# Four entries ordered by gathers through HBM, and the perceptron's bias and mask on TensorE and ScalarE

## The chip, the cores and the metric

The kernel runs on one core of one Trainium2 chip. The time is the device time of one execution in microseconds; the median of several executions is given. The profile is that of one execution.

## What is computed

There are 16 graphs ("entries") of 1024 nodes with 64 features, and a dense weighted adjacency matrix for each. Four layers follow one another; each adds its result to x and normalises the 64 features.

```
layer 0: messages = adj @ x;  dh = tanh([x, messages] @ W1 + b1) @ W2 + b2
layer 1: (adj / rowsum(adj)) @ x
layers 2, 3: neighbours are thinned by their rank, symmetrically
         for each node and feature, over the values of its remaining neighbours:
             agg = 0.25*quantile(.25) + 0.5*quantile(.5) + 0.25*quantile(.75)
         y = (relu((x + agg) @ W1 + b1) @ W2 + b2) * mask
after each layer: x = layernorm(x + result)
```

## The kernel before

The work of an entry is split into stages, each a Python generator. `features` does layers 0 and 1 on TensorE from adjacency columns that SyncE loads 512 KB at a time, twice per entry. `cuts` finds the neighbours to be removed. `lists` makes the reduced neighbour matrix, counts each node's neighbours and ranks the nodes by that count; `order` is the permutation as a 0/1 matrix of 1024 x 1024. All later work is on nodes in this order, so that the nodes of one tile of 128 have similar counts and tile t needs at most SIZES[t] values for each node.

Still in `lists` (L802 to L865) every tile but the last is packed: for tile t the rows of the neighbour matrix that belong to it are selected with `order` (16 matmuls of 512 columns, L861 to L863, after two that add a position term, L860), and from the result `pk` ScalarE and VectorE read off the neighbours' numbers, `e.idx`. The last tile (`by_pick`) is packed the other way round (L851 to L855). `ordered` (L867) selects each node's count, number and mask with `order` (`ps`), orders x2 with 192 matmuls on a three-part bf16 copy of it (`pick`, L882 to L886, from `x2p` made by `split` in `features`, L637 to L639), copies the result to `x2s` and stores it in a DRAM table.

`fetch` then gathers, with one indirect DMA of GpSimd for each list position, 128 rows of that table into a ring of 60 slots, `got_s`. VectorE sorts the slots by compare-exchange steps, ScalarE scales the wanted ones by quantile weights (`weigh`), TensorE adds them up. For the last tile and the longest lists, TensorE selects the values with 0/1 matrices instead (`mark_picks`, `fill`: hot, pgk). A round takes two entries through one layer; the 16 rounds are (layer, pair) = (0,0), (0,1), (1,0), (0,2), (1,1), (0,3) and so on. `finish` (L1162) is a round's end for one entry: four groups of two tiles through the perceptron, then the layer norm, then the table of the next layer or the scatter of the output.

The order of the instructions on VectorE, ScalarE and TensorE is that in which the generators issue them. `Weave` always resumes the generator whose next time is earliest, on the clock of `Clocks`, a planner with fixed costs for each engine (L238) that keeps when each tile is written and read; `landed` and `vacant` hold a generator back until the plan says that data is there or room is free. `clocks.put` also charges the queues of SyncE and GpSimd. The engines themselves work through their queues in order and wait on semaphores. Entries are prepared one after another; `allowed` lets the preparation run ahead of the rounds, first to entry 4.

Two lines that the text refers to:

```
L884  pick(px[:, t, :], order[:, :, t * P : (t + 1) * P], e.x2p)
L1184 dve.tensor_add(y[:, g : g + 2], pd, b2r[:, None, :].to_broadcast([P, 2, C]))
```

In the profile every instruction of this part stands under L301, the line of the wrapper that records it, so groups are told apart by their tiles.

Of the kernel before, what the change touches and what calls it, by code (L numbers as in the profile page):

```python
# [22 lines left out]
P = 128  # L23
# [13 lines left out]
HALVINGS = 0  # L37
ROOM = 60
BY_PICK = 6
LONG = 40  # L40
BIG = 1e30
EPS = 1e-5
# [283 lines left out]
def adj_resnorm_kernel(ctx: ExitStack, tc: tile.TileContext, x, adj_t, nodemask, w01, b01, w02, b02,  # L326
                       w21, b21, w22, b22, w31, b31, w32, b32, out):
    nc = tc.nc
    B, N, C = x.shape
    NT = N // P  # L330
# [5 lines left out]
    s = SimpleNamespace()  # L336
# [38 lines left out]
        nc.vector.memset(ends_of[:, i : i + 1], float(value))  # L375
    one_f = const.tile([P, 1], F32, name="one_f")
    nc.vector.memset(one_f, 1.0)
    eps = const.tile([P, 1], F32, name="eps")
    nc.vector.memset(eps, EPS)
    nth = const.tile([P, 1], F32, name="nth")  # L380
# [90 lines left out]

    table = [[dram.tile([N + 1, C], F32, name=f"table{layer}{i}") for i in range(TABLES)] for layer in range(2)]
    table_t = dram.tile([C, N], F32, name="table_t")
    with tc.tile_pool(name="last_row", bufs=1) as last_row:
        no_row = last_row.tile([1, C], F32, name="no_row")
        nc.vector.memset(no_row, BIG)
        for tab in table[0] + table[1]:
            nc.sync.dma_start(tab[N : N + 1, :], no_row)
# [66 lines left out]
    def features(b, e):  # L545
# [32 lines left out]
        for h in range(NH):  # L578
# [6 lines left out]
            for q in range(G):  # L585
                t = h * G + q
# [47 lines left out]
        yield from settle(x2, y, "x")  # L634
        while b and entries[b - 1].xs[0] is None:
            yield
        parts = s.feat.tile([P, NT, 3, C], BF, name="x2p", bufs=1)  # L637
        yield from split(x2, parts, y)
        e.x2p = parts  # L639
# [79 lines left out]
    def lists(b, e):  # L719
# [29 lines left out]
        for t in range(NT + 1):  # L749
            if t:  # L750
                bank, pv = pvs[t - 1]
                nc.scalar.activation(left(t - 1), pv, AF.Relu, accum_out=key[:, 4, t - 1 : t], saturate=False)
                read_big[bank] = True
            if t < NT:
                rows = slice(t * P, (t + 1) * P)
                bank, pv = yield from big("pv")
                pvs.append((bank, pv.rearrange("p (c n) -> p c n", n=P)))
                for h in range(NH):
                    wide = slice(h * HALF, (h + 1) * HALF)
                    nc.tensor.matmul(pv[:, wide], minus_i, takes[:, t, wide], start=True, stop=False)  # L760
                    for c in range(h * G, (h + 1) * G):
                        cols = slice(c * P, (c + 1) * P)
                        nc.tensor.matmul(pv[:, cols], near[:, c, rows], ident_b, start=False, stop=False)
                        nc.tensor.matmul(pv[:, cols], takes[:, c, rows], minus_i, start=False, stop=c == (h + 1) * G - 1)
            yield
# [33 lines left out]

        e.idx = s.feat.tile([P, LINKS[-1]], I32, name="idx", bufs=6)  # L800
        pks, codes, found = {}, {}, {}
        for t in (*reversed(range(NT)), -1, -2, -3, -4):  # L802
            done = t + 4
            if done in found:
# [43 lines left out]
            if t >= 0:  # L848
                rows = slice(t * P, (t + 1) * P)
                bank, pk = pks[t] = yield from big("pk")  # L850
                if t in e.by_pick:  # L851
                    for q in range(NT):
                        for c in range(NT):
                            nc.tensor.matmul(pk[:, q * P : (q + 1) * P], left(c, q), order[:, c, rows],
                                             start=c == 0, stop=c == NT - 1)  # L855
                else:
                    for h in range(NH):
                        wide = slice(h * HALF, (h + 1) * HALF)
                        cols = pk[:, wide].rearrange("p (q n) -> p q n", n=P)
                        nc.tensor.matmul(pk[:, wide], first_ones, minus_at[:, wide], start=True, stop=False)  # L860
                        for c in range(NT):  # L861
                            nc.tensor.matmul(cols, order[:, c, rows], left(c, slice(h * G, (h + 1) * G)), start=False,
                                             stop=c == NT - 1)  # L863
                e.packed = t == 0
            yield  # L865

    def ordered(b, e, order, own):  # L867
# [9 lines left out]
        sorted_own = s.work.tile([P, NT, 3], F32, name="sorted_own", bufs=1)  # L877
        nc.scalar.copy(sorted_own, ps)
        count = sorted_own[:, :, 0]
        while e.x2p is None:  # L880
            yield
        px = s.psum.tile([P, NT, C], F32, name="ordered_x", tag="s", bufs=1)  # L882
        for t in range(NT):
            pick(px[:, t, :], order[:, :, t * P : (t + 1) * P], e.x2p)  # L884
            if t % 2:
                yield  # L886
        e.out_rows = s.feat.tile([P, NT], I32, name="out_rows", bufs=8)
        dve.tensor_scalar(e.out_rows, sorted_own[:, :, 1], float(b * N), None, op0=ALU.add)
        e.mask = s.feat.tile([P, NT], F32, name="mask_s", bufs=8)
        dve.tensor_copy(e.mask, sorted_own[:, :, 2])  # L890
        yield
        while b >= 4 and entries[b - 4].xs[1] is None:
            yield
        e.xs[0] = s.feat.tile([P, NT, C], F32, name="x2s", bufs=4)
        nc.scalar.copy(e.xs[0], px)
        nc.sync.dma_start(table[0][b % TABLES][:N, :].rearrange("(t p) c -> p t c", p=P), e.xs[0])
        weave.add(parted(b, e, 0))
        places = {}
# [263 lines left out]
    def finish(m, b, e, layer, agg, spare=False):  # L1162

        xc = e.xs[layer]
        w1s, b1c, w2s, b2r = mlps[layer]
        own, wide = ("y_x", "node_in") if spare else ("y_m", "o_t")

        y = s.work.tile([P, NT, C], F32, name="y_m", tag=own, bufs=1)
        own_rows = slice(m * C, (m + 1) * C)
        for g in range(0, NT, 2):  # L1170
            if spare:
                bank = s.psum.tile([P, N], F32, name="m_o", tag="big", bufs=2)
            else:
                bank = s.psum.tile([P, HALF], F32, name="m_o", tag="m", bufs=1)
            ph, pd = bank[:, : 2 * P], bank[:, 2 * P : 3 * P].rearrange("p (g c) -> p g c", c=C)
            nc.tensor.matmul(ph[:H], w1s[own_rows], agg[own_rows, g : g + 2, :], start=True, stop=True)
            yield
            h_t = s.work.tile([H, 2 * P], F32, name="h_t", tag=wide, bufs=1)
            nc.scalar.activation(h_t, ph[:H], AF.Relu, bias=b1c)
            yield  # L1180
            for q in range(2):
                nc.tensor.matmul(pd[:, q, :], h_t[:, q * P : (q + 1) * P], w2s, start=True, stop=True)
            yield
            dve.tensor_add(y[:, g : g + 2], pd, b2r[:, None, :].to_broadcast([P, 2, C]))  # L1184
        dve.tensor_mul(y, y, e.mask[:, :, None].to_broadcast([P, NT, C]))
        dve.tensor_add(y, y, xc)
        tag, bufs = ("x3s", 4) if layer == 0 else ("x2s", 4) if spare else ("x4s", 1)
        xn = s.feat.tile([P, NT, C], F32, name="xn", tag=tag, bufs=bufs)
        yield from settle(xn, y, "x" if spare else "m")
        yield  # L1190
        if layer == 0:
            nc.sync.dma_start(table[1][b % TABLES][:N, :].rearrange("(t p) c -> p t c", p=P), xn)
            e.xs[1] = xn
            weave.add(parted(b, e, 1))
            return
        for t in range(NT):
            put = nc.gpsimd.indirect_dma_start(
                out=out_rows_of, out_offset=bass.IndirectOffsetOnAxis(ap=e.out_rows[:, t : t + 1], axis=0),
                in_=xn[:, t, :], in_offset=None)
            tc.declare_no_dep(put.ins, group=f"rows{b}", reason="they write different rows")  # L1200
            tc.add_to_no_dep_group(f"rows{b}", put.ins)
# [43 lines left out]
    def landed(*aps):  # L1245
        while clocks.when(*aps) > clocks.now:
            yield clocks.when(*aps) + SLACK

    def quiet(engine, ahead=0.5):
        while clocks.free[engine] > clocks.now + ahead:  # L1250
            yield clocks.free[engine] - ahead / 2

    entries = [SimpleNamespace(near=None, st=None, cut=False, taken=False, packed=False, listed=None, there=None, by_pick=(NT - 1,), place6=None, seated=(), placed=False, counted=False, x2p=None, place=None, none=None,
                               wts=None, parts=[None, None], xs=[None, None], filled=[False, False], ends=None) for _ in range(B)]
    for e in entries:
        e.listed, e.there, e.seated = set(), {}, set()
# [462 lines left out]
```

## Time and profile before

| | |
|---|---|
| median of 3 runs | 7080.39 us (7067.44 to 7087.93) |
| the profiled execution | 7089.6 us, its span 7087.9 us |
| mean granted TensorE clock | 0.721 |
| gathers into the ring (POOL) | 2872, 1027 ns each |
| x2s written, entries 0 to 3 | at 179, 444, 700 and 926 us |
| x2s written, entries 4 and 5 | at 1327 and 1559 us |
| mask multiplied in finish, round 0 | at 929 and 1053 us |
| the same, round 1 | at 1676 and 1802 us |

PE is TensorE's matmuls, PEld its weight loads, which overlap them; DVE is VectorE, ACT ScalarE, POOL GpSimd, SP SyncE. A group in the profile is written out<-in with the names of the tiles, and x is the number of instructions. A float32 matmul stands as two instructions. Busy shares are means over the whole run. In waits, "issue" is idle time for which the profile shows no cause, and "remote" a release that it can't attribute. Some matmul records can be missing from a trace.

### The profile page before, as it was taken

How to read it: one execution, taken by the hardware profiler on the slowest of the kernel's cores; microseconds unless marked ns; L12 is line 12 of the kernel's file. 1: busy time of each engine (PE TensorE's matmuls, PEld its weight loads, DVE VectorE, ACT ScalarE, POOL GpSimd, SP SyncE). 2: the span in 40 equal slices, each digit the busy share in tenths (PEclk: the TensorE clock that was granted, in tenths of full speed). 3: DMA queues.
4: the chain of work that ended last, by engine and by line, in shares of the span. 5: the costliest groups of instructions: out<-in, count | busy, mean ns of one | idle time of the engine just before them, and what ended most of it. 6: DMA issues, size and time to landing. Idle time of an engine off the chain costs nothing.

```text
span 7087.9 us, 127458 instructions
## 1 busy us (share of the span) xinstructions
PE 4478.5 (63%) x51916; PEld 3422.8 (48%) x51916; DVE 4036.7 (57%) x8753; ACT 3112.9 (44%) x7225; POOL 3090.2 (44%) x3096
## 2 busy tenths in 40 slices
PE   7678676776665767566675656657666566454354
PEld 5446444554544545454544535545555454353344
DVE  2447345574654747556564655638465477375646
ACT  4446444454434445444443444445343444233233
POOL 0432225535254454544455354544445454455540
PEclk8678776776776867777776767768677677666667
DMA  2212212221111211111121211201111010001100
GB/s 79 49 38 60 53 44 49 51 50 20 36 45 24 57 21 46 40 40 41 24 51 29 52 27 30 56 18 39 44 42 32 16 20 16 17 18 21 18 15 5
DMA packets 414449, 253.93 MB, mean 36 GB/s; under 512 B 103434, under 2 KB 365850, under 8 KB 413850
## 3 DMA queue, kind: packets, MB, share of 16 engines
q0 software_dynamic: 96000, 98.50, 7.8%
q1 hardware_dynamic: 317850, 147.19, 7.3%
q8 instruction: 408, 6.68, 0.4%
q14 instruction: 191, 1.56, 0.1%
HBM read 232.88 MB, written 12.59 MB: 35 GB/s over the span
## 4 chain that ended last, share of the span: by engine, by line
PE 41%; issue 21%; DVE 15%; ACT 12%; another core or an unknown queue 9%; POOL 1%; DMA 0%; DVEq 0%; ACTq 0%; POOLq 0%
PE pgk L301 19%; PE pk L301 7%; DVE other L301 6%; DVE got_s L301 4%; PE pa L301 3%; ACT junk L301 2%; ACT hot L301 2%; DVE got L301 2%; PE px L301 2%; PE pr L301 2%; PE m_o L301 2%; ACT got_s L301 2%; PE ordered_x L301 1%; ACT got L301 1%
## 5 line engine op out<-in xcount | busy, mean ns | idle before, releaser
L301 POOL DMA_INDIRECT got_s<-table,idx x2872 | 2948.2, 1027 | 3707.0 <-DVE other L301 1096.4
L301 PEld LDWEIGHTS <-hot 128*128 128x128 bf16 x26304 | 1172.9, 112 | 1686.2 <-issue 1480.2
L301 PE MATMUL pgk<-x1p,hot 128*128 128x64 bf16 x13152 | 709.3, 216 | 692.1 <-issue 499.8
L301 PE MATMUL pgk<-x0p,hot 128*128 128x64 bf16 x13152 | 693.0, 214 | 676.9 <-issue 545.4
L301 DVE TENSOR_SCALAR hot<-place 128x1024 bf16<-128x1024 f16 (+1 forms) x824 | 320.8, 428 | 974.4 <-remote 769.3
L301 PEld LDWEIGHTS <-order 128*128 128x128 bf16 x7008 | 392.1, 105 | 520.0 <-issue 384.9
L301 ACT COPY got<-pgk 64x192 f32<-64x192 f32 (+2 forms) x600 | 182.5, 305 | 994.7 <-PE pgk L301 797.5
L301 ACT COPY agg<-pgk 128x128 f32<-128x128 f32 (+2 forms) x183 | 44.3, 242 | 1164.8 <-PE pgk L301 708.1
L301 PE MATMUL pk<-near,order 128*128 128x512 fp8e4 x1760 | 490.3, 418 | 55.2 <-issue 51.9
L301 DVE TENSOR_TENSOR other<-got_s 128x512 f32<-128x512 f32 (+10 forms) x826 | 491.5, 607 | 13.4 <-DVE hot L301 0.3
L301 PE MATMUL pgk<-ident,got_s 128*64 128x128 f32 x2904 | 425.4, 326 | 89.8 <-ACT got L301 36.2
L301 PEld LDWEIGHTS <-near 128*128 128x128 fp8e4 x4224 | 300.1, 109 | 302.9 <-issue 301.5
L301 PEld LDWEIGHTS pgk<-ident,got_s 128*64 128x64 f32 x2904 | 386.9, 167 | 119.9 <-ACT got L301 41.2
L301 ACT ACTIVATE got_s<-got_s,wts 128x64 f32<-128x64 f32 x1540 | 391.1, 335 | 95.0 <-DVE got_s L301 86.5
L301 DVE TENSOR_TENSOR got_s<-other 128x512 f32<-128x512 f32 (+9 forms) x719 | 391.4, 559 | 8.2
L301 DVE TENSOR_TENSOR got_s<-got_s 128x512 f32<-128x512 f32 (+9 forms) x638 | 373.0, 589 | 20.8 <-ACT got_s L301 5.4
L301 PE MATMUL pa<-x,adj_r 128*128 128x65 f32 x2048 | 331.5, 320 | 78.4 <-issue 70.9
L301 PEld LDWEIGHTS pa<-x,adj_r 128*128 128x128 f32 x2048 | 318.9, 238 | 92.1 <-issue 85.5
L301 ACT ACTIVATE code<-pk,ends_of 128x1024 f16<-128x1024 f32 x220 | 235.4, 1106 | 255.7 <-PE pk L301 113.2
L301 DVE TENSOR_TENSOR other<-other 128x128 f32<-128x128 f32 (+10 forms) x617 | 323.1, 524 | 17.8
L301 ACT ACTIVATE junk<-pr,nb_st 128x1024 fp8e4<-128x1024 f32 x256 | 284.7, 1112 | 72.7 <-remote 34.5
L301 ACT ACTIVATE hot<-hot,one_f 128x1024 bf16<-128x1024 bf16 x272 | 312.3, 1148 | 8.9
(211 smaller groups left out, 7779.9 us busy)
## 6 DMA issues: line engine op xcount, KB each, us to landing
adj_r<-in_adj_dram SPq DMA_DIRECT2D x256, 512.0 KB
got_s<-table,idx POOLq DMA_INDIRECT x2872
x_s<-in_x_dram SPq DMA_DIRECT2D x16, 256.0 KB
table<-x2s SPq DMA_DIRECT2D x16, 256.0 KB
table<-xn SPq DMA_DIRECT2D x16, 256.0 KB
out_dram<-xn,out_rows POOLq DMA_INDIRECT x128
table<-no_row SPq DMA_DIRECT2D x12, 0.2 KB
w21s<-in_L_gnn_W_dram SPq DMA_DIRECT2D x2, 32.0 KB
```

The costliest lines, as they stand in the source:

```text
L301: return call(*args, **kwargs)
```

## The change

For the first four entries (EARLY = 4) the selection of rows by matmuls with `order` is replaced by gathers through HBM, in two places. The reduced neighbour matrix is stored to DRAM (`left_d`), one store of 128 KB for each of its 8 parts, in runs of 128 bytes; the sorted node numbers are made an index (`from_rows`); for each tile but the last, one indirect DMA fetches its 128 rows of 1 KB, two tiles ahead, and one matmul for each half with the identity brings them into `pk` beside the position term. x2 is stored to DRAM (`x2_d`), and 8 indirect DMAs write `x2s` directly. The three-part split and the 192 matmuls for these entries are gone.

In `finish`, for all entries and both layers, the perceptron's second bias is added by a float32 matmul with one contraction row (`ones_row` and one row of the bias) that opens the accumulation for each tile; the mask is multiplied by ScalarE as it copies each tile out of PSUM. The two VectorE steps (the addition of the bias for each group, the multiplication by the mask for the entry) are gone.

```
@@ features
+        if b < EARLY:
+            nc.sync.dma_start(x2_d[b].rearrange("(t p) c -> p t c", p=P), x2)
+            e.x2p = x2
+            return
         parts = s.feat.tile([P, NT, 3, C], BF, name="x2p", bufs=1)
         yield from split(x2, parts, y)
@@ lists
                 nc.scalar.activation(left(t - 1), pv, AF.Relu, accum_out=key[:, 4, t - 1 : t], saturate=False)
+                if b < EARLY:
+                    to = left_d[b][(t - 1) * P : t * P, :]
+                    nc.sync.dma_start(to.rearrange("p (q n) -> p q n", n=P // 4), left(t - 1).bitcast(F32))
...
+        def fetch_row(t):
+            gather(fetched_rows[:, t % 2], left_d[b], e.from_rows[:, t : t + 1])
+        if b < EARLY:
+            fetched_rows = s.feat.tile([P, 2, N // 4], F32, name="fetched_rows", tag="x3s", bufs=4)
+            while e.from_rows is None:
+                yield
...
+                    if b < EARLY:
+                        yield from landed(fetched_rows[:, t % 2])
                     for h in range(NH):
                         nc.tensor.matmul(pk[:, wide], first_ones, minus_at[:, wide], start=True, stop=False)
+                        if b < EARLY:
+                            nc.tensor.matmul(pk[:, wide], ident_b, fetched_rows[:, t % 2].bitcast(F8)[:, wide], start=False, stop=True)
+                            continue
                         for c in range(NT):
                             nc.tensor.matmul(cols, order[:, c, rows], left(c, slice(h * G, (h + 1) * G)), start=False,
                                              stop=c == NT - 1)
+                if b < EARLY:
+                    if t == NT - 1:
+                        fetch_row(t - 1)
+                        fetch_row(t - 2)
+                    elif t > 1:
+                        fetch_row(t - 2)
@@ ordered
+        if b < EARLY:
+            e.from_rows = s.feat.tile([P, NT], I32, name="from_rows", bufs=2)
+            dve.tensor_copy(e.from_rows, sorted_own[:, :, 1])
...
+        if b >= EARLY:
+            px = s.psum.tile([P, NT, C], F32, name="ordered_x", tag="s", bufs=1)
+            for t in range(NT):
+                pick(px[:, t, :], order[:, :, t * P : (t + 1) * P], e.x2p)
...
+        if b >= EARLY:
+            nc.scalar.copy(xs, px)
+        else:
+            yield from landed(x2_d[b][:])
+            for t in range(NT):
+                gather(xs[:, t, :], x2_d[b], e.from_rows[:, t : t + 1])
+            yield from landed(xs)
@@ finish
             for q in range(2):
-                nc.tensor.matmul(pd[:, q, :], h_t[:, q * P : (q + 1) * P], w2s, start=True, stop=True)
-            yield
-            dve.tensor_add(y[:, g : g + 2], pd, b2r[:, None, :].to_broadcast([P, 2, C]))
-        dve.tensor_mul(y, y, e.mask[:, :, None].to_broadcast([P, NT, C]))
+                nc.tensor.matmul(pd[:, q, :], ones_row, b2r[:1], start=True, stop=False)
+                nc.tensor.matmul(pd[:, q, :], h_t[:, q * P : (q + 1) * P], w2s, start=False, stop=True)
+            yield
+            for q in range(2):
+                nc.scalar.activation(y[:, g + q, :], pd[:, q, :], AF.Copy, scale=e.mask[:, g + q : g + q + 1])
+        yield
```

More of the change, by code (lines that the diff above doesn't have):

```diff
@@ L39 @@
 BY_PICK = 6
+EARLY = 4
 LONG = 40
@@ L377, in adj_resnorm_kernel @@
     nc.vector.memset(one_f, 1.0)
+    ones_row = const.tile([1, P], F32, name="ones_row")
+    nc.vector.memset(ones_row, 1.0)
     eps = const.tile([P, 1], F32, name="eps")
@@ L473, in adj_resnorm_kernel @@
     table_t = dram.tile([C, N], F32, name="table_t")
+    left_d = [dram.tile([N, N // 4], F32, name=f"left_d{b}") for b in range(EARLY)]
+    x2_d = [dram.tile([N, C], F32, name=f"x2_d{b}") for b in range(EARLY)]
     with tc.tile_pool(name="last_row", bufs=1) as last_row:
@@ L879, in ordered @@
         count = sorted_own[:, :, 0]
-        while e.x2p is None:
-            yield
[L882 to L886, printed above, removed]
+        if b < EARLY:
+            e.from_rows = s.feat.tile([P, NT], I32, name="from_rows", bufs=2)
+            dve.tensor_copy(e.from_rows, sorted_own[:, :, 1])
         e.out_rows = s.feat.tile([P, NT], I32, name="out_rows", bufs=8)
@@ L890, in ordered @@
         dve.tensor_copy(e.mask, sorted_own[:, :, 2])
+        while e.x2p is None:
+            yield
[3 more added lines that the diff above has]
+                pick(px[:, t, :], order[:, :, t * P : (t + 1) * P], e.x2p)
+                if t % 2:
+                    yield
         yield
@@ L893, in ordered @@
             yield
-        e.xs[0] = s.feat.tile([P, NT, C], F32, name="x2s", bufs=4)
-        nc.scalar.copy(e.xs[0], px)
+        xs = s.feat.tile([P, NT, C], F32, name="x2s", bufs=4)
+        if b >= EARLY:
[5 more added lines that the diff above has]
+            yield from landed(xs)
+        e.xs[0] = xs
         nc.sync.dma_start(table[0][b % TABLES][:N, :].rearrange("(t p) c -> p t c", p=P), e.xs[0])
@@ L1181, in finish @@
             for q in range(2):
-                nc.tensor.matmul(pd[:, q, :], h_t[:, q * P : (q + 1) * P], w2s, start=True, stop=True)
+                nc.tensor.matmul(pd[:, q, :], ones_row, b2r[:1], start=True, stop=False)
+                nc.tensor.matmul(pd[:, q, :], h_t[:, q * P : (q + 1) * P], w2s, start=False, stop=True)
             yield
-            dve.tensor_add(y[:, g : g + 2], pd, b2r[:, None, :].to_broadcast([P, 2, C]))
-        dve.tensor_mul(y, y, e.mask[:, :, None].to_broadcast([P, NT, C]))
+            for q in range(2):
+                nc.scalar.activation(y[:, g + q, :], pd[:, q, :], AF.Copy, scale=e.mask[:, g + q : g + q + 1])
+        yield
         dve.tensor_add(y, y, xc)
@@ L1251, in quiet @@
             yield clocks.free[engine] - ahead / 2
-    entries = [SimpleNamespace(near=None, st=None, cut=False, taken=False, packed=False, listed=None, there=None, by_pick=(NT - 1,), place6=None, seated=(), placed=False, counted=False, x2p=None, place=None, none=None,
+    entries = [SimpleNamespace(near=None, st=None, cut=False, taken=False, packed=False, listed=None, there=None, by_pick=(NT - 1,), place6=None, from_rows=None, seated=(), placed=False, counted=False, x2p=None, place=None, none=None,
                                wts=None, parts=[None, None], xs=[None, None], filled=[False, False], ends=None) for _ in range(B)]
```

## The prediction

> **What bounds the kernel now.** I read the page first, then the waits, then the start of the run in the chain and in windows, because the larger half of the change acts only there.
>
> ```profile
> PE 4478.5 (63%) x51916; PEld 3422.8 (48%) x51916; DVE 4036.7 (57%) x8753; ACT 3112.9 (44%) x7225; POOL 3090.2 (44%) x3096
> ...
> PE 41%; issue 21%; DVE 15%; ACT 12%; another core or an unknown queue 9%; POOL 1%; DMA 0%; DVEq 0%; ACTq 0%; POOLq 0%
> ```
>
> No engine looks full, but the chain runs over PE for 41%, and 21% is "issue", time without a visible cause. The waits say whose it is (engine, releaser, total us, times, longest):
>
> ```profile
> POOL got_s L301 <- DVE other L301: 1096.4, 74, 87.7
> PE pgk L301 <- issue: 1088.6, 1293, 10.1
> ...
> DVE hot L301 <- remote: 769.3, 93, 54.0
> ...
> PE pgk L301 <- ACT got L301: 383.2, 140, 29.8
> DVE y_m L301 <- PE m_o L301: 334.9, 66, 25.3
> ```
>
> PE's waits on named others are 664 us for ACT and 234 us for DVE in the whole run, 13% of 7088. The rest of its idle time, 1638 us, is "issue". So PE is held by its own stream for about 87% of the span, while DVE and ACT stand behind it (DVE waits 335 us for the perceptron's matmuls alone). Two windows at the start show what such "issue" time is:
>
> ```profile
> core 0: us, PE busy (x) PEld busy (x) DVE busy (x) ACT busy (x) POOL busy (x), PEclk, DMA share, GB/s
> 149.00:195.00 46.00, 46.00 (x461) 28.42 (x459) 20.34 (x32) 23.98 (x35) 5.99 (x7) 1.00 0.21 56
> 196.00:254.00 58.00, 5.05 (x40) 3.31 (x39) 0.00 (x0) 0.28 (x1) 38.67 (x41) 0.53 0.14 24
> ```
>
> From 149 to 195 us, entry 0 is put in order: PE is full at clock 1.00, POOL hardly works. From 196 POOL gathers back to back (41 in 58 us), PE gets 40 matmuls through, ACT and DVE nothing. The trace gives no cause, but the neighbourhood is plain: a gather can cost PE up to 58/41 = 1.4 us. On average it is at most 1638/3000 = 0.55 us (2872 gathers, 128 scatters).
>
> The chain from 150 us gives the prices of what is removed:
>
> ```profile
> 150.03 1.40 PE ordered_x L301 x48
> 151.44 1.00 PE px L301 x2
> 152.44 4.30 PE pk L301 x18
> ```
>
> One block of 18 matmuls packs one tile of an entry; four blocks of 48 order x2.
>
> **What the Trainium skill says.** "TensorE: Matmul & The Clock Gate", section "LDWEIGHTS (loading the stationary operand)": the load's time goes by columns, not by rows of the contraction. The trace agrees: m_o's weights of 64 rows load in 182 ns at least, those of 128 rows in 186. So a bias matmul with a single row is priced as a full one. Its section "Architectural detail: the array is 16× 32×32, not 1× 128×128": matmuls keep program order, only weight loads are pulled ahead; so one that waits for a fetched row holds all behind it. The window from 196 us agrees at least in that nothing else got past. "DMA: Bandwidth & Descriptors", "Anatomy of one DMA — SWDGE (gpsimd) path": about 2 us fixed, mostly the write's receipt, HBM the heaviest. Here the 256 KB store of table (issued 181.47) let the first gather go at 187.18, 5.7 us later, so I use 5.7. Its "Specifications": full rate needs 512 bytes or more; the new stores have runs of 128 bytes, and no run here shows such a store.
>
> **The change, part by part.** The sum is made against the profiled execution, 7089.6 us (span 7087.9 and 1.7 around it), which is 9 us above the median of 7080.4; the difference is then taken from the median.
>
> *Packing of entries 0 to 3.* Seven tiles each, 28 in all, go from 18 matmuls to 4. At 4.30 us per 18, 4 cost 0.96; saved 3.34 x 28 = 94 us at full clock. The granted clock from 0 to 930 us, in which these four entries are prepared, is 0.77: 94/0.77 = 121 us of PE.
>
> *Ordering of x2.* Four blocks of 1.40 us per entry: 5.6 x 4 = 22 us, 29 at 0.77. The split of x2 goes too: 3 copies of 0.62 us on ACT, 2 subtractions of 0.69 on DVE, 13 us in all. Costed at nothing: from 0 to 930 us ACT is 51% and DVE 45% busy, behind PE; 13 us if PE no longer covers it.
>
> *Gathers.* 7 rows of 1 KB and 8 of x2 per entry, 60 in all. On POOL 1.25 us apart (0.94 and a gap of 0.30): 75 us on an engine busy for 236 of those 930. Their price on PE isn't known for these shapes: between 0 and 1.4 us each, 0 to 84 us; by the bytes (28 of them carry four times the usual) 0 to 144 x 1.4 = 202. A gain is excluded, since nothing shows PE faster beside gathers. I take 0.55 x 60 = 33, because most come singly between packing steps, not in bursts of 40.
>
> *Stores.* 36 more DMAs on SP, 32 of 128 KB and 4 of 256. An adjacency load queued behind a left_d store waits for ACT's Relu. Loads run two tiles ahead, and PE waited for one DMA, 9.7 us once, at the start. Cost 0; if that cover goes, a few us for each of 32. The x2_d store lands long before its gathers.
>
> *New waits on PE.* A tile's matmul waits for its row. Behind it stand features, picks and cuts of other entries in PE's queue, and behind PE stand ACT and DVE. Rows are fetched two tiles ahead; a tile takes about 8 us now (152.44, 159.17, 167.20, 174.79 in the chain), so a fetch has some 12 us. The store is over by then, and I take 5.7 us as enough for gather and landing: hidden, 0. Ends: 0 to 8.5 us for each row of entries 1 to 3 (below). For x2s, 8 gathers (10 us) and 5.7 stand in place of 25 us of picking: no loss. Waiting for from_rows before the first tile adds the ps matmuls and two copies, 2 us, under other work.
>
> Start, together: -121 - 29 + 33 = -117 us of PE, times the 0.87 that PE carries: **-102**.
>
> *Bias on PE.* From the last round:
>
> ```profile
> 7043.91 1.10 PE L301 MATMUL m_o<-w32s,h_t 128*128 128x64 f32 x8 [0.62 <-ACT h_t L301]
> 7044.67 0.29 DVE L301 TENSOR_TENSOR y_m<-m_o,b32r 128x128 f32<-128x128 f32 x1 [1.69 <-PE m_o L301]
> ```
>
> That line has two entries' group of two tiles: 8 instructions, 4 per entry, 0.55 us. The bias adds as many: 4 groups x 0.55 = 2.2 us in a finish, 70 in 32 at full clock, 98 at the mean clock of 0.721; I take 84. 22 finishes lie before 5800 us (0.87 carried), 10 after it, where PE is only half busy (0.5): 84 x (0.69 x 0.87 + 0.31 x 0.5) = **+63**. Bounds 35 and 98.
>
> *Bias and mask off DVE, onto ACT.* DVE loses 128 x 0.29 + 32 x 0.69 = 59 us and, more, its stand before m_o (335 us, and part of 169 put down to "remote"). ACT gets 256 scalings at 0.25 us (8 in 2.0 us in the last layer norm), 64 us, and that stand. Behind DVE's stand were sorting and picks' marks; behind ACT's are the emptying of pick banks and scaled rows. PE waits 234 us for DVE and 664 for ACT, so the swap lies between -234 and some +100 (15% of 664). DVE also feeds POOL's slots (1096 us). I take **-15**.
>
> *The very end.* Four groups get 0.5 us on ScalarE and 0.55 on PE for one DVE add of 0.29 (about +0.75 each), and the mask's 0.69 goes: **+2**.
>
> Sum: -102 + 63 - 15 + 2 = -52: 7038 for the profiled execution, **7028** for the median. What is late next: still PE, now with perceptron work spread over all rounds.
>
> **Rivals.**
> *The rows come late* (slower, 7122). POOL works in order too, and waits 14.8 us on average (1096.4/74) for a sort to free a slot; a fetch behind such a wait stops PE. Of the lead of 12 us the gather takes 5.7, so 14.8 - 6.3 = 8.5 us are left; for every second of the 21 rows of entries 1 to 3 that is 11 x 8.5 = +94. It decides from 52/8.5, six rows. For: POOL's long waits. Against: in entry 0 POOL has nothing else, and slots are freed by the work that PE has already passed.
> *The start doesn't set the pace* (slower, 7130). If rounds 0 and 1 are paced by sorting, or the planner's new order wastes the room, -102 vanishes and +63 - 15 + 2 stays: +50. For: round 0's first finish comes only at 929 us, round 1's at 1676. Against: PE is as full there as before it.
> *DVE was worth more* (7028 - 102 = 6926). If half of PE's 234 us for DVE goes, the swap is -117. For: DVE stands 335 us before m_o. Against: most of those stands end when PE arrives, and PE isn't sped up by them.
>
> **Numbers.** Forecast 0.52 (own range 6985 to 7075, from the bounds of gathers and bias), rows late 0.15, start hidden 0.13, DVE more 0.20. About 0.3%, 21 us, is what a measurement can tell from no change: faster 0.40 of the forecast and 0.20 of the last, 0.60; same 0.12 + 0.02 = 0.14; slower 0.15 + 0.11 = 0.26. The range reaches to 6920 and, past the late rows and the hidden start, to 7140; it leaves out the upper halves of these two and the low tail of the last.
>
> **What would show it.** Right: pk and ordered_x cost PE some 150 us less before the fourth x2s, which comes at about 820 us instead of 926; PE doesn't wait for fetched_rows; m_o has 512 more instructions; "DVE y_m <- PE m_o" is gone and ACT has it. Wrong: waits of PE for POOL's rows of over 52 us in all, the fourth x2s no earlier, or the lead at 926 us gone again by the end of round 1 (1802).

## The result and the profile after

The changed kernel takes **7204.49 us** (median of 4, 7168.87 to 7219.08), the kernel before 7084.16 in the same comparison: ratio 1.0166, 95% interval 1.0142 to 1.019, or +120 us. The forecast was 7028 and its range ended at 7140. The profiled execution took 7204.08 us, its span 7202.4, its mean granted clock 0.704 (before 0.721).

The page of the changed kernel, busy time and the clock by slices:

```profile
PE 4564.8 (63%) x51268; PEld 3532.1 (49%) x51268; DVE 3989.1 (55%) x8590; ACT 3168.4 (44%) x7469; POOL 3150.9 (44%) x3156
...
PEclk7667667777867767677676877768676777666666
```

TensorE has 648 matmul records fewer than before and yet 86 us more busy time. VectorE lost 48 us of busy time and ScalarE got 56: the direction is that of the edit, which by the forecast's count takes 59 us from VectorE and brings ScalarE 64. The waits of the changed kernel (engine, releaser, total us, times, longest):

```profile
PE pgk L302 <- issue: 1005.7, 1211, 13.0
POOL got_s L302 <- DVE other L302: 999.6, 72, 96.3
...
DVE hot L302 <- PE pgk L302: 468.2, 199, 26.3
...
PE pgk L302 <- ACT got L302: 336.5, 122, 29.9
...
DVE y_m L302 <- ACT y_m L302: 121.5, 14, 30.4
...
PE m_o L302 <- ACT y_m L302: 50.4, 23, 9.9
```

and a row of the kernel before:

```profile
DVE hot L301 <- PE pgk L301: 191.7, 108, 20.9
```

"DVE y_m <- PE m_o" is gone, as forecast. VectorE has not been freed by it: it now stands before TensorE's pick results ("hot <- pgk") for 468 us, 192 before. The last row shows a new wait: TensorE's next perceptron matmul waits until ScalarE, no longer VectorE, has emptied the bank (a part of PSUM, where TensorE's results stand).

The times at which x2s is stored show where the lead should have been (us, in the profiled executions; "gathers alone" is the start's part of the change without the perceptron's):

| store of x2s | 1st | 2nd | 4th | 6th | 10th | 16th |
|---|---|---|---|---|---|---|
| before | 181 | 445 | 926 | 1559 | 3249 | 5756 |
| after | 162 | 411 | 920 | 1642 | 3255 | 5829 |
| gathers alone | 161 | 415 | 925 | 1630 | 3200 | 5782 |

The second is 34 us earlier, the fourth 6 us, not 106. The sixth is 83 us later, but that is no loss by itself: the planner's new order puts rounds ahead of preparation. The two finishes of round 1 add x2s at 1510 and 1643 us, before at 1676 and 1803. At the end the span is 114 us longer.

### The profile page after: what moved, and what is told of

It reads as the page before. It is cut to its first block, busy times and chain, and to the rows that moved or that the text cites. A ratio compares the mean times of both kernels' runs of the same rounds, so it can differ in the third digit from the quotient of the medians.

```text
span 7202.4 us, 126358 instructions
## 1 busy us (share of the span) xinstructions
PE 4564.8 (63%) x51268; PEld 3532.1 (49%) x51268; DVE 3989.1 (55%) x8590; ACT 3168.4 (44%) x7469; POOL 3150.9 (44%) x3156
## 5 line engine op out<-in xcount | busy, mean ns | idle before, releaser
L302 PEld LDWEIGHTS <-hot 128*128 128x128 bf16 x26304 | 1209.5, 114 | 1584.2 <-issue 1353.0
L302 PE MATMUL pgk<-x0p,hot 128*128 128x64 bf16 x13152 | 727.0, 219 | 670.5 <-issue 501.9
L302 PEld LDWEIGHTS <-order 128*128 128x128 bf16 x5792 | 323.0, 104 | 424.3 <-issue 320.7
L302 PE MATMUL pa<-x,adj_r 128*128 128x65 f32 x2048 | 357.9, 335 | 116.0 <-issue 109.6
L302 PEld LDWEIGHTS pa<-x,adj_r 128*128 128x128 f32 x2048 | 344.4, 254 | 134.3 <-issue 123.4
L302 PE MATMUL pk<-near,order 128*128 128x512 fp8e4 x1312 | 360.8, 422 | 11.4 <-issue 10.9
L302 DVE TENSOR_TENSOR other<-other 128x64 f32<-128x64 f32 (+10 forms) x617 | 323.9, 525 | 18.7
L302 ACT ACTIVATE hot<-place,minus_k 128x1024 bf16<-128x1024 f16 (+1 forms) x272 | 310.7, 1142 | 18.8 <-remote 12.8
```

The costliest lines, as they stand in the source:

```text
L302: return call(*args, **kwargs)
```

## The experiments

Two parts of the planner's apparatus are used below. An instruction issued through `whole` goes to its engine without being charged to the planner; `clocks.put` (or `ghost`, which only calls it) charges the planner for an instruction that isn't issued. So the order of all other instructions can be kept as in one kernel while the instructions of another are run. "Dead" matmuls are overwritten by the true ones.

The runs were made on several chips, and the chips are of two kinds: on three of them the kernel before takes 7087, 7096 and 7197 us, on two 4841 and 4844. What differs is told under the observations. Each difference below is that of the medians from the kernel before on the same chip, the ratio is given with its 95% interval; **P** marks chips of the first kind, on which the result was measured, **Q** the second.

### Which half loses

`gathers_only` (P) is the changed kernel with the perceptron of before:

```
-                nc.tensor.matmul(pd[:, q, :], ones_row, b2r[:1], start=True, stop=False)
-                nc.tensor.matmul(pd[:, q, :], h_t[...], w2s, start=False, stop=True)
+                nc.tensor.matmul(pd[:, q, :], h_t[...], w2s, start=True, stop=True)
             yield
-            for q in range(2):
-                nc.scalar.activation(y[:, g + q, :], pd[:, q, :], AF.Copy, scale=...)
-        yield
+            dve.tensor_add(y[:, g : g + 2], pd, b2r[...])
+        dve.tensor_mul(y, y, e.mask[...])
```

> The changed kernel with the old finish: only the gathers through HBM for the first four entries. Theory 'perceptron': the start gains next to nothing, because PE's granted clock fell in the first 800 us (0.72 and 0.68 against 0.75 and 0.77) as its work fell, and the whole loss is the perceptron's: 7084 +- 30. The prediction's own sum for this half was -102, so 6980. Rival 'gathers': the fetched rows cost the +120: over 7150.

7084.11 against 7095.66, ratio 0.9987 (0.9974 to 1.0), -12. `finish_only` (P) is the other half, the kernel before with the new perceptron:

> The kernel before with the new finish: bias on PE, mask on ACT, no gathers. Theory 'perceptron': +90 to +130, 7175 to 7215. The prediction's sum for this half was +50 (63 - 15 + 2), so 7134. Rival 'gathers': within 30 us of before.

7231.85, ratio 1.0187 (1.0165 to 1.0208), +136, a little above the expected +130. The loss is the perceptron's, and the start brings next to nothing.

An edit changes the instructions and, through the planner, the order of everything else. Two kernels part these. `finish_old_plan` (P) has the new instructions in the order of before:

```
+                whole.tensor.matmul(pd[:, q, :], ones_row, b2r[:1], start=True, stop=False)
...
+            clocks.put("DVE", "tensor_add", (...), {})
+            for q in range(2):
+                whole.scalar.activation(y[:, g + q, :], pd[:, q, :], AF.Copy, scale=...)
+        clocks.put("DVE", "tensor_mul", (...), {})
```

> The new finish's instructions, but the planner is charged for the old ones, so that all other instructions keep the order of the kernel before. If the instructions themselves cost the time: nearly all of what finish_only loses, +80 to +120. If it is the planner's new order: within 25 us of before.

7229.07, 1.0185 (1.0158 to 1.0213), +133, again a little above. `finish_new_plan` (P) has the old instructions in the order that the planner makes for the new ones:

> The old finish's instructions, but the planner is charged for the new ones, so that all other instructions have the order of finish_only. If the instructions cost the time: within 25 us of before. If the new order does: nearly all of what finish_only loses, +80 to +120.

7111.4, 1.0018 (1.0006 to 1.0031), +16. So the instructions themselves cost it; the new order adds at most some tenths of a per cent. Both halves were run once more beside the next pair, on another chip of kind P:

> gathers_only again, beside the three below on one chip. The first four runs and the second four came from two chips on which the kernel before takes 7096 and 4841 us, so parts can only be summed within a chip. If the gathers are worth nothing on either: within 30 us of before.

7085.57 against 7086.98, 0.9995 (0.9983 to 1.0008), -1.

> finish_old_plan again: on the chip of 7096 us +133 was measured; if the next two add up, the sum of both; on a chip of 4841 us 59 + 71 = +130.

7213.59, 1.0167 (1.0146 to 1.0189), +127.

### Bias or mask

`bias_pe` moves only the bias to TensorE. VectorE multiplies each group by the mask out of PSUM in place of the addition; the order is that of before.

```
+                whole.tensor.matmul(pd[:, q, :], ones_row, b2r[:1], start=True, stop=False)
...
+            clocks.put("DVE", "tensor_add", (...), {})
+            whole.vector.tensor_mul(y[:, g : g + 2], pd, e.mask[:, g : g + 2, None]...)
+        clocks.put("DVE", "tensor_mul", (...), {})
```

On Q:

> The kernel before, in its own order (the planner is charged for the old finish), with the bias alone on PE; VectorE multiplies each group of two tiles by the mask straight from PSUM. If the 512 new PE instructions cost the time: +80 to +130, most of finish_old_plan's +133 (m_o's PE busy time rose by 155 us there). If ScalarE's stand before m_o does: +63 at most, the prediction's price for the bias, and mask_act takes the rest.

4903.01 against 4841.13, 1.0121 (1.0103 to 1.014), +62: below the first range, at the edge of the second. On P:

> bias_pe again: +59 was measured on the chip of 4841 us. If PE's 512 instructions cost their PE time on either chip: +50 to +90.

7178.78 against 7086.98, 1.0134 (1.0094 to 1.0173), **+92**.

`mask_act` moves only the mask to ScalarE, which copies out of PSUM with the scale; no bias is added by anyone. On Q:

> The kernel before, in its own order, with the mask on ScalarE, two scalings for each group straight from PSUM, and no second bias at all (left out). If PE's instructions cost the time: within 30 us of before. If ScalarE's stand and its later release of the m_o bank do (PE waited 85 us for y_m on ScalarE in finish_old_plan, 19 us for y_m on VectorE before): +50 to +90.

4911.99, 1.0144 (1.0127 to 1.0161), +71: so on Q both parts cost. On P:

> mask_act again: +71 was measured on the chip of 4841 us, with PE waiting 111 us for y_m on ScalarE at the next group's first matmul, against 26 us for VectorE in bias_pe. If that wait is the cost: +50 to +90 on either chip.

7134.18, 1.0062 (1.0045 to 1.0078), **+47**, just below the range. On P the two parts add up to 139, beside 127 to 136 for both together. The waits of `mask_act_b`:

```profile
DVE y_m L301 <- ACT y_m L1186: 251.8, 27, 24.4
...
PEld m_o L301 <- ACT y_m L1186: 115.8, 44, 16.2
PE m_o L301 <- ACT y_m L1186: 106.8, 40, 16.1
```

and the row of the kernel before that stood in the place of the last:

```profile
PE m_o L301 <- DVE y_m L301: 19.1, 13, 5.6
```

VectorE stands before y_m as it did, now for ScalarE (252 us; 335 before). New is that TensorE waits 107 us in 40 places, 19 in 13 before, for the perceptron's bank to be emptied. Two scalings of 0.31 us each stand in ScalarE's queue behind whatever is there, where VectorE needed one step of 0.29.

What the bias costs can be read off a single group. The timeline of `bias_pe` in its first round, then that of `pack_doubled` (below), whose perceptron is that of before; both on Q at full clock (start, duration, engine, instructions merged):

```profile
711.92 0.29 PEld L1184 LDWEIGHTS m_o<-b22r,ones_row 1*128 1x128 f32 x2
711.92 0.43 PE L1184 MATMUL m_o<-b22r,ones_row 1*128 1x64 f32 x2
...
712.28 0.30 PEld L301 LDWEIGHTS m_o<-w22s,h_t 128*128 128x128 f32 x2
712.28 0.44 PE L301 MATMUL m_o<-w22s,h_t 128*128 128x64 f32 x2
712.65 0.29 PEld L1184 LDWEIGHTS m_o<-b22r,ones_row 1*128 1x128 f32 x2
...
713.01 0.30 PEld L301 LDWEIGHTS m_o<-w22s,h_t 128*128 128x128 f32 x2
...
713.37 0.30 PEld L301 LDWEIGHTS px<-adj_r,x_s 128*64 128x64 f32 x3
```

```profile
766.73 0.53 PEld L301 LDWEIGHTS m_o<-w22s,h_t 128*128 128x128 f32 x4
766.75 0.64 PE L301 MATMUL m_o<-w22s,h_t 128*128 128x64 f32 x4
...
767.32 0.41 PEld L301 LDWEIGHTS px<-adj_r,x_s 128*64 128x64 f32 x4
```

Without the bias the four loads of a group follow each other 0.11 us apart, and the next work begins after 0.59 us. With it, a pair's first load begins no earlier than its own first matmul and 0.36 us after the pair before; the group takes 1.45 us. Eight instructions cost not twice the four but two and a half times. That is 0.86 us for each group in place of the forecast 0.55.

`bias_bf16` (Q) asks whether this price is what the time follows: one bf16 matmul with one row in place of the float32 pair.

```
+                whole.tensor.matmul(pd[:, q, :], ones_b, b2_b[:, layer, :], start=True, stop=False)
```

> The bias on TensorE as one bf16 matmul with one row (the bias rounded to bf16), instruction order of before, mask on VectorE for each group: 256 instructions added to TensorE instead of 512. bias_pe with its float32 pair gave +92 on one chip and +62 on another. If the cost goes by the number of instructions on TensorE: half of that, +30 to +50. If it goes by one more dependent step (PSUM bank taken earlier, mask for each group on VectorE): as much as bias_pe.

4867.65 against 4844.11, 1.0053 (1.0036 to 1.007), +24. Its timeline:

```profile
712.65 0.20 PE L1187 MATMUL m_o<-b_b,ones_b 1*128 1x64 bf16 x1
...
712.78 0.43 PE L301 MATMUL m_o<-w22s,h_t 128*128 128x64 f32 x2
713.14 0.09 PEld L1187 LDWEIGHTS <-ones_b 1*128 1x128 bf16 x1
```

A tile takes 0.49 us (712.65 to 713.14), against 0.73 with the float32 bias and 0.29 without. The added work is 0.20 and 0.44 us, the added time +24 and +62: a little below the +30 expected, nearer to the work than to a fixed price of one more dependent step, which would have given the same 62.

### Where the start's 102 us went

`pack_cut2` (Q) keeps the selection of entries 0 to 3 to one of its eight chunks, with the planner still charged for all:

```
+                            if b < 4 and c:
+                                clocks.put("PE", "matmul", (...), {})
+                                continue
```

> The kernel before, in its own order, without 14 of the 18 matmuls of each packed tile of entries 0 to 3 (the selection is over one of eight chunks, so the lists are wrong, and the sentinel for absent values is 1e8): PE's relief alone, no gathers, no new order. If PE holds 87% of the time, as the prediction had it: -80 to -120. If the start's PE work is not what sets the end: within 25 us of before, and the fourth x2s hardly earlier than 926 us.

4867.76, 1.0046 (1.0032 to 1.006), +27, near the second statement; the fourth x2s comes at 765 us, in `mask_act`, on the same chip, at 742. The end can't be read: with the wrong lists the gathers of the rounds are another load (their queue takes 18.3% of the DMA engines' time, in `mask_act` 9.6%, for the same bytes). The clock from 0 to 760 us is 0.78, in `mask_act` 0.86, though no gather was added.

`pack_doubled` (Q) is the kernel before with the 16 selecting matmuls of each packed tile of entries 0 to 3 issued a first time, dead:

```
+                        for c in range(NT if b < 4 else 0):
+                            whole.tensor.matmul(cols, order[:, c, rows], left(c, ...),
+                                                start=c == 0, stop=c == NT - 1)
                         nc.tensor.matmul(pk[:, wide], first_ones, minus_at[:, wide], start=True, stop=False)
```

> The kernel before, with the 16 selecting matmuls of each packed tile of entries 0 to 3 issued twice (the first time dead), in the order of before; no gather is added. It adds 28 x 16 matmuls, 107 us at full clock. If TensorE's own stream sets the pace in the start: +90 to +139. If the start does not set the pace: within 25 us of before. If work that runs without a pause raises the granted clock enough to pay for part of itself: +30 to +80.

4928.81 against 4844.11, 1.0177 (1.016 to 1.0194), **+85** for 107 us of full-clock work, just short of the +90 of the first theory. TensorE's work in the start does count.

`gathers_padded` puts the same dead matmuls into `gathers_only`. It was run twice on Q:

> gathers_only in its own order, with the 16 selecting matmuls of each packed tile put back as dead work (their result is overwritten): the gathers without PE's relief. If PE's work in the start counts: +80 to +120 over gathers_only. If the relief was worth nothing there: within 25 us of gathers_only, with the granted clock in the first 930 us back from 0.70 towards 0.77.

4907.79, 1.0134 (1.0118 to 1.0151).

> gathers_only plus 16 dead selecting matmuls ahead of each packed tile of entries 0 to 3, so TensorE has all the work that the gathers were to spare, and the gathers as well. Theory 'gathers eat it' (the spared 94 us of TensorE at full clock are real, and the 60 gathers, their waits and the lower clock cost as much again): 90 to 130 us above gathers_only. Theory 'the start does not set the pace': within 25 us of gathers_only.

4910.7, 1.0134 (1.0117 to 1.0151), +67. Beside the second ran

> The start's part of the change alone (old perceptron), as a baseline beside the next three. All theories: within 0.2% of before, as twice measured (0.9987, 0.9995).

4861.85, 1.0041 (1.0027 to 1.0056), +18, more than the 0.2% expected. The 107 us put back cost 49 with the gathers, between the two theories. The windows from 0 to 760 us of `pack_doubled`, `gathers_only_c` and `gathers_padded_b` (busy us of PE, PEld, DVE, ACT, POOL, then the granted clock):

```profile
0.00:760.00 760.00, 636.05 (x6342) 458.88 (x6360) 403.67 (x1087) 437.00 (x889) 240.56 (x328) 0.87 0.25 65
```

```profile
0.00:760.00 760.00, 605.55 (x6613) 480.46 (x6628) 476.25 (x1257) 519.98 (x1078) 356.26 (x436) 0.81 0.36 88
```

```profile
0.00:760.00 760.00, 637.20 (x6429) 469.74 (x6445) 440.85 (x1172) 493.26 (x1011) 319.82 (x404) 0.87 0.33 81
```

With the dead work the clock is 0.87, without it 0.81. The clock falls as the work is taken away. The Trainium skill, "TensorE: Matmul & The Clock Gate", section "What's actually happening", says that the throttled state is the default and that sustained activity releases it; these windows agree in direction. The two kernels with the gathers issue everything else in the same order, so their stores of x2s can be compared: without the dead work the fourth comes 38 us earlier (687 against 725), the sixth 56 (1175 against 1231), the sixteenth 59 (3904 against 3963). On Q the relief lasts to the end. Still `gathers_only_c` is 18 us slower than before.

Is it the planner's order that costs what the relief brings? `gathers_new_plan` (P) runs the start of before, selection and ordering on TensorE and no gathers, in the order that the planner makes for the gathers:

```
-            gather(fetched_rows[:, t % 2], left_d[b], e.from_rows[:, t : t + 1])
+            ghost.gpsimd.indirect_dma_start(out=fetched_rows[:, t % 2], ...)
...
+                            ghost.tensor.matmul(pk[:, wide], ident_b, fetched_rows[...], ...)
+                            for c in range(NT):
+                                whole.tensor.matmul(cols, order[:, c, rows], left(c, ...), ...)
```

> The instructions of the kernel before (selection and ordering on TensorE, no gather, no store of left or x2), in the order that the planner makes when it is told of the gathers. Theory 'the new order loses it' (told of room on TensorE in the start, the planner lets rounds and preparation change places, and the later order is worse): 50 to 90 us above before. Theory 'the gathers lose it' (their traffic and their waits): within 25 us of before. gathers_padded, with nearly the same order and TensorE work and the gathers as well, was 66 us above before.

7200.77 against 7197.0, 1.0002 (0.9989 to 1.0015). In the traces the work common to both runs on TensorE, VectorE and ScalarE in the order of `gathers_only`; the sixth and the sixteenth x2s are stored at 1659 and 5920 us, later than before, and the time is that of before. `gathers_old_plan` (P) has the gathers while the planner is still charged for the matmuls that are gone:

> gathers_only, but the planner is still told of the selecting and ordering matmuls, the split and the copy that are gone, so it does not fill the room on TensorE; gathers and stores are charged as in gathers_only. Theory 'the new order loses it': the lead of the fourth x2s lasts and the time is 30 to 80 us below before. Theory 'the gathers lose it': as gathers_only, 0 to 20 us above before.

7211.54, 1.0029 (1.0012 to 1.0045). This is not the order of before, since the gathers are charged as well: round 1 ends at 1657 us here, at 1615 in `gathers_only` and at 1803 before. It shows only that a third order saves nothing either. `gathers_new_plan` decides: on P the new order alone costs nothing, so what stands in place of the selection and the ordering (gathers, stores, a lower clock) costs as much as it spares. How, is in the first 930 us of three kernels on P; the header is that of all such windows. Before:

```profile
core 0: us, PE busy (x) PEld busy (x) DVE busy (x) ACT busy (x) POOL busy (x), PEclk, DMA share, GB/s
0.00:930.00 930.00, 666.95 (x6682) 492.17 (x6683) 423.05 (x1131) 470.59 (x949) 236.15 (x328) 0.77 0.21 55
```

`gathers_new_plan`, the same instructions in the new order:

```profile
0.00:930.00 930.00, 670.86 (x6624) 498.29 (x6640) 419.08 (x1133) 464.10 (x948) 236.43 (x328) 0.76 0.20 55
```

`gathers_only`:

```profile
0.00:930.00 930.00, 620.36 (x5835) 480.71 (x5835) 415.63 (x1130) 459.12 (x939) 288.98 (x384) 0.70 0.26 65
```

The gathers spare TensorE 47 to 51 us of busy time, not 150. By an estimate from these two clocks the same work would have taken 620 x 0.70/0.77 = 564 us at the clock of before, so 56 us went into the lower clock. And TensorE's waits of the kind "issue" in this window add up to 136 us before, 114 in `gathers_new_plan`, 186 in `gathers_only`: 50 to 73 more. Less busy and more "issue" cancel, and the fourth x2s comes when it did (925 us, 926 before).

The added "issue" time does not stand beside the new gathers. Within 1.25 us of the start of one of them (the distance of two gathers in a row) there are 13 us of it in `gathers_only`; beside the 232 gathers of the rounds there are 151, in `gathers_new_plan` 92, before 120. In those same 290 us TensorE is busy for 174 us in `gathers_new_plan`, 49 of them with selecting matmuls, and for 129 in `gathers_only`. So about half of the 94 us that the selection takes by 930 us in `gathers_new_plan` lay beside gathers that are there in either kernel; with the selection gone TensorE is idle there instead.

## Why the prediction was wrong

| term | forecast | measured on P |
|---|---|---|
| start (gathers for packing and ordering) | -102 | -12 and -1 |
| bias on TensorE | +63 | +92 |
| mask to ScalarE, VectorE freed | -15 | +47 |
| very end | +2 | +1.5 |
| sum | -52 | +120 (measured as a whole) |

The very end is already within the measured times of bias and mask. The other three make 127 to 138, the whole 120. The ratios' intervals of bias and mask alone reach some 28 and 12 us to either side.

**Packing and ordering, -121 and -29.** Two steps failed. One is the division by a clock taken as fixed ("94/0.77"). The spared instructions are gone from the trace as counted (the selecting matmuls from 1760 records to 1312, ordered_x from 3072 to 2304). But the granted clock of the stage fell from 0.77 to 0.70, by which the work that stayed got longer, by the estimate 56 us. That the clock follows the work in the stage was shown on Q by putting the work back (0.81 to 0.87). The other is the factor 0.87: it counts "issue" as TensorE's own stream, so that all spared work shortens the run. About half of the selection lay beside the rounds' gathers, and "issue" took its place.

**Gathers, +33.** "Issue" grew by 50 to 73 us where 33 was taken, inside the bound of 84. But a price for each new gather is the wrong form: only 13 us stand beside the 56 new ones of this window, 0.2 us each. The forecast's "most come singly" was wrong too: in `gathers_only` 10 to 12 of the 15 of an entry follow one another about 1.25 us apart. Why TensorE waits longer beside the old ones was not shown beyond what is said above.

**Waits on PE for rows, 0.** Right, and with it the first rival falls. The rows of the changed kernel, what they wait for and who waits for them:

```profile
L302 PE MATMUL pk<-fetched_rows,ident_b x56: 389/390/610, 152.0 to 987.7; 128*128 128x512 fp8e4 x56
L302 POOL DMA_INDIRECT fetched_rows<-left_d,from_rows x28: 943/948/1293, 147.7 to 956.3; - x28
its engine sat idle before it (us, times) until:
  DVE mask_s L302: 216.4, 3
...
who waited for it (us, times):
  POOL fetched_rows L302: 87.5, 14
  ACT code L302: 3.5, 5
```

POOL stood idle ahead of them until their numbers were there (216 us in three places, put down to DVE's copy into mask_s, which follows the one into from_rows), and no wait of TensorE for the rows is listed. So no run here shows whether a late row would have held up all behind it. The stores, costed at 0, were not tried by themselves; what they cost is in the start's sum. The prediction's "one DMA, 9.7 us once, at the start" was misread: before, TensorE waits for DMAs three times, 22.7 us in all, the 9.7 at 830 us; after, 13.3 us.

**"The start doesn't set the pace".** Its number, 7130, was the nearest, and its sign right: the start's term vanished. Its reason was wrong on Q, where 107 us of added work in the start made the whole 85 us longer: there TensorE sets the pace. On P work was not added, and with half of the selection beside gathers the reason may hold in part. That the new order wastes the room is refuted on P by `gathers_new_plan`.

**Bias, +63.** The mechanism was right and the size too small. The failed term is "the bias adds as many: 4 groups x 0.55". A group takes 0.86 us more, 128 of them 110 us at full clock instead of 70. m_o's busy time on TensorE is 309.3 us in `bias_pe` and 180.2 in `pack_doubled` on Q, 366 in `bias_pe_b` and 214 before on P: +129 and +152 where 84 was taken. With the forecast's own share of 0.75 that would be +97 and +114; measured +62 and +92. So the work was taken too small and its share somewhat too large, about 0.5 on Q and 0.6 on P. The Trainium skill's section "LDWEIGHTS (loading the stationary operand)" was read rightly for one load: in `bias_pe` 184 ns in the median with one row and 189 with 128. What was overlooked is that the four loads of before start 0.11 us apart, and that with one-row pairs between them each pair starts 0.36 us after the one before. The clock hid a part too: the block of 8 from which the 0.55 was read took 1.10 us at full clock, and two blocks later the same 8 took 1.97 at half clock; in `bias_pe_b` the last block of 16 takes 5.0.

**Mask and bias off VectorE, -15.** Wrong in sign, inside its bounds. The trade was to be worth what TensorE waits for each engine. The failed term is "DVE loses ... its stand before m_o": in `mask_act_b` VectorE still stands 252 us at the next step of y_m, now for ScalarE, and TensorE's waits for VectorE are 225 us (234 before). Its waits for ScalarE rose from 664 to 694 in sum, and those for the emptying of the perceptron's bank by 88. In the prediction's text the new wait was named for VectorE and the pick banks, but not the nearest one: the next group's first matmul needs the bank that ScalarE now empties. But most of those 88 us took the place of other waits. The profiled executions differ by 39.5 us: TensorE waits some 19 us more for the two engines together, and its busy time is 22 us longer at a clock of 0.717 (0.721 before). So that the bank's wait is the price is argued, not shown by itself, and the 22 us were not separated.

**"DVE was worth more", 6926.** Not borne out: of the 234 us that TensorE waits for VectorE 9 went in the same run, not half.

**The very end, +2.** In `finish_old_plan_b` 12.8 us pass from the start of the last two h_t to the first scatter of the output (7173.69 to 7186.47), before 11.3 (7049.15 to 7060.43).

**The marks named in advance.** m_o has its 512 more instructions, "DVE y_m <- PE m_o" is gone and TensorE waits for no row: these held. pk and ordered_x take 103 us less in the first 930 us (56 and 0 instead of 135 and 25), not 150. The fourth x2s at 820 didn't come; it came 6 us early, which had been named as a sign that the prediction is wrong. The other sign, the lead gone by the end of round 1, tells nothing here: under the new order that round ends 160 us earlier and the sixth x2s comes 83 us later, and `gathers_new_plan`, without gathers, does nearly the same (1644 and 1659 us).

What stays open: on Q, with about 1 us of "issue" time in the start, the relief is worth 49 us to the end, and yet the start's part of the change costs 18 us. Whether gathers, stores or the new order take the difference there isn't settled, since `gathers_new_plan` was run on P alone. That the lower clock in the start is a consequence of the spared work, and not of the pauses that gathers bring, is shown on Q only; that the longer "issue" time on P follows from the spared work too is read from where it stands, and no run tried it. None of the kernels is faster than the one before beyond the measurement; the start's part alone is equal to it on P.

## What to carry to other kernels

Work taken off a busy TensorE isn't worth its time at the clock of before: look whether the stage is left with enough work to keep that clock, and whether the work stood in time in which the engine is held up anyway. A small matmul put between large ones costs more than its own length if it breaks a run of weight loads that follow one another closely; price it as the length of the whole group with it, and at the clock at which most of the groups run. Before a copy out of PSUM is moved to another engine, look who needs the bank next, and what stands ahead of the copy in the new engine's queue.

## What the runs showed of the hardware

**Two kinds of chips.** The same instructions of the kernel before take 7084 to 7197 us on some chips and 4841 to 4844 on others. On the first, TensorE's waits without a visible cause ("issue") are 1638 us; in `pack_doubled` on a chip of the second kind they are 8. While the first 41 gathers of the rounds run, TensorE is busy for 13 of 51 us in `bias_pe_b` on P and for 46 of 53 in the same kernel on Q (`bias_pe`). So the slowing of TensorE beside gathers, from which the prediction took its price, belongs to the chip and not to the kernel. What in the chip makes it isn't known from these runs.

**One row between 128.** Float32 matmuls of one shape started 0.11 us apart (median in `pack_doubled`). When pairs with 1 row and pairs with 128 rows alternate, the starts are 0.16 us apart within a pair and 0.20 from pair to pair, and a pair takes 0.36 us (`bias_pe`, at full clock). One bf16 matmul with a row costs 0.20 us of the tile's time in the same place.

**Gathers of 1 KB rows** take POOL no longer than those of 256 bytes: 948 ns in the median for fetched_rows, 947 for the gathers of x2s in the changed kernel.
